# Window attention on one core: values multiplied over 128 rows of keys, and bands fetched at another place in the queue

## The chip, the core and the metric

The kernel runs on one core of a Trainium2 chip. Its time is the device time of one execution in microseconds (us); the time before is the median of three runs, 4207.44 us (4202.64 to 4210.01). A profile is one further execution with the hardware profiler on. Engines are named as in it: PE is TensorE's matmuls, PEld its weight loads, DVE is VectorE, ACT ScalarE, POOL GpSimd, and SP SyncE, which here only issues DMAs.

## What is computed

Two layers on `x` of 16 images, 56 x 56 pixels, 384 channels, all in float32. Cut to what matters:

```python
# layer 0: group norm, then shifted-window attention: windows of 7 x 7 pixels, 12 heads of 32 channels
qkv = roll(gn(x), (-3, -3)) @ w_qkv.T
score = einsum('bhwqd,bhwkd->bhwqk', q, k) / sqrt(32) + rel      # per window: 49 x 49
# the last row and the last column of windows: -inf between the shifted parts
out = einsum('bhwqk,bhwkd->bhwqd', softmax(score), v)
x = x + roll(out @ w_out.T + b_out, (3, 3))
# layer 1: group norm, then a 3 x 3 depthwise convolution with weights -1, 0 or 1
x = x + depthwise3x3(gn(x), sign(w))
```

## The kernel before, in words

**Strips and units.** An image is cut into 8 strips of 7 rows, which are 8 windows each (128 strips in all). A strip is two units of 4 windows, so there are 256 units. For each strip, TensorE multiplies the normalized input `xn` with the weights: queries and keys (`query_key`, L472), values (`value`, L485), and after attention the output projection (`project`, L656). Tokens lie along the free axis there, 392 at a time, and the shape is 128 x 128 weights. Results go to four PSUM banks (`bank`, L91) used in turn, and are copied out by ScalarE (L479, L492) or VectorE (L664).

**Attention of a unit.** The four windows are two pairs: `r` counts pairs, `w` the window in a pair. Window `w` of a pair has its keys in partitions 64 w to 64 w + 48. `scores` (L526) multiplies keys and queries, 48 matmuls of 32 rows; VectorE scales them and adds bias and mask into the tile `e` (`softmax`, L543); ScalarE makes the exponentials in place, with their sum along a row into `reach` for a later range check (`exponential`, L561). `add_up` (L597) sums over keys by a matmul with ones, `invert` makes the reciprocal on ScalarE and VectorE (L635 to L638), `attend` (L617) multiplies values and exponentials, one window and one head at a time, ScalarE copies the two banks `po` out (L627), and `divide` (L645) multiplies with the reciprocals. A float32 matmul is two passes in the records, each with its own weight load: the 48 matmuls of `attend` are 96 instructions.

```python
keys = slice(w * HT, w * HT + T)          # HT 64, T 49, D 32
nc.tensor.matmul(
    po[w][i * D : (i + 1) * D, (2 * j + r) * T : (2 * j + r + 1) * T],
    vs[s][keys, n * 2 + r, h * D : (h + 1) * D],
    by_head(u)[keys, i * NC + j, r] if fast else pts[u, j][keys, 2 * i + r, :],
```

The values get keys on partitions by 32 x 32 transposes on VectorE (`turn`, L496) and 16 DMAs a strip from SP (`by_key`, L508), which each carry a semaphore that the first matmuls of the strip wait for.

**The convolution** of image b - 1 runs beside the attention of image b. Its input goes to DRAM (`mid`, L680) and comes back in bands of 28 rows of one channel block, six to an image. For each band: `band` (L703) fetches it on SP into the one buffer `xb`; `pad` (L748) and `middle` (L778) on ScalarE normalize it into a padded tile and start the sum; eight `tap`s on VectorE (L784) add to it; `turn_sum` (L791) transposes, and eight `store`s (L798) send it from SP. The last image has no attention beside it: there a part of the channels is convolved on TensorE (`convolve`, L822, `carry`), the rest goes through `turn_late` (L855 to L863).

**The order.** Every engine takes its instructions in the order in which the program writes them. `all_units` writes, for each unit, six steps of large matmuls (`heavy`) with the attention's parts between them: `add_up`, `invert`, `attend` and `divide` after the first; `scores` and `softmax` of the next unit after the third or fourth (in the first or second unit of a strip), its `exponential` after the step that follows. All else has a due time in units (`at`), and is written when the unit comes to it. `plan_conv` gives the bands their due times: `step` is 2.6 units, `lead` is 3, and a band is due 0.75 steps before its first tap, its pad 0.35, its middle 0.25. One SP queue carries value loads, bands and stores in this order.

A second pass of the whole kernel, with `fast` false, runs only where the range check asks for it; it doesn't for these inputs.

Of the kernel before, what the change touches and what calls it, by code (L numbers as in the profile page):

```python
# [9 lines left out]
F32 = mybir.dt.float32  # L10
I32 = mybir.dt.int32
AF = mybir.ActivationFunctionType
# [22 lines left out]
def kernel(  # L35
# [55 lines left out]
    def bank(name):  # L91
        return ps.tile([P, 512], F32, tag="mm", name=name)
# [6 lines left out]
    ones = const.tile([P, P], F32, tag="ones", name="ones")  # L99

    least = const.tile([P, 1], F32, tag="least", name="least")
    reach = const.tile([P, 2, B * NU], F32, tag="reach", name="reach")
    seen = const.tile([P, B + NC], F32, tag="seen", name="seen")
    again = const.tile([P, 1], I32, tag="again", name="again")
    wq_t = const.tile([P, NC, 3 * C], F32, tag="wq", name="wq_t")
# [11 lines left out]

    xt = const.tile([P, NC, NR, D], F32, tag="xt", name="xt")

    es = const.tile([P, NH, 2, HT], F32, tag="e", name="e")  # L120

    hps = [const.tile([P, BR + 2, W + 2], F32, tag=f"hp{n}", name=f"hp{n}") for n in range(2)]

# [14 lines left out]
    def clear_more():  # L138
        nc.gpsimd.memset(power, -0.5)
        nc.gpsimd.memset(ones, 1.0)  # L140
        nc.gpsimd.memset(least, LEAST)
        nc.gpsimd.memset(seen, 0.0)
        for t in (qk[:, :, ST:], *hps, *accs):
            nc.gpsimd.memset(t, 0.0)
# [45 lines left out]
    def load_bias(queue, first_q, last_q, fast):  # L190


        if not loaded_bias:
            rel = ypool.tile([P, NC, WIN, R], F32, tag="y", name="rel").rearrange("q c h w -> q (c h w)")[:, : T * NH]
            nc.gpsimd.memset(rel, 0.0)
            loaded_bias.append(rel)
        rel = loaded_bias[0]
        flat = rel.rearrange("q (a n) -> q a n", a=WIN)
        for q in range(first_q, last_q):
            qr, qc = divmod(q, WIN)  # L200
            first = qr * REL + qc if fast else (WIN - 1 - qr) * REL + (WIN - 1 - qc)
            row = rel_table[first : first + 1, :]
            src = bass.AP(
                tensor=row.tensor,
                offset=row.offset,
                ap=[[NH, 1], [REL * NH, WIN], [1, WIN * NH]],
            )
            queue.dma_start(flat[q : q + 1], src)
        if last_q < T:
            return  # L210
        queue.dma_start(flat[HT : HT + T], flat[0:T])
        mask = ypool.tile([P, NC, WIN, R], F32, tag="y", name="mask").rearrange("q c h w -> q (c h w)")[:, : 2 * T]
        mask = mask.rearrange("q (v k) -> q v k", v=2)
        nc.gpsimd.memset(mask, 0.0)
        for w in range(2):
            queue.dma_start(mask[w * HT : w * HT + T], wmask[0:T, :, 0:T])
        loaded_bias.append(mask)
# [317 lines left out]
    def softmax(u, fast):  # L535

        s = u // UPS
        pp = raw[u]
        e = es.rearrange("k (i j) w q -> k i (j w) q", i=HPC)[:, :, :, :T]
        if fast:  # L540
            flat = es.rearrange("k h w q -> k (h w q)")[:, : NH * 2 * T]
            e = flat.rearrange("k (i n q) -> k i n q", i=HPC, q=T)
        nc.vector.scalar_tensor_tensor(  # L543
            e,
            pp[:, :, : NC * 2 * T].rearrange("q i (n k) -> q i n k", k=T),
            QSCALE,
            bias[:, int(s % NS == NS - 1)].rearrange("q (i j) w k -> q i (j w) k", i=HPC),
            ALU.mult,
            ALU.add,
        )  # L550
        if fast:
            return
        e = es.rearrange("q h w k -> q (h w) k")[:, :, :T]
        top = small.tile([P, 2 * NH], F32, tag="top", name=f"top_{u}")
        nc.vector.tensor_reduce(top, e, AX.X, ALU.max)
        nc.vector.tensor_tensor(e, e, top.unsqueeze(2).to_broadcast([P, 2 * NH, T]), ALU.subtract)

    def exponential(u, fast):
        if fast:
            flat = es.rearrange("k h w q -> k (h w q)")[:, : NH * 2 * T]  # L560
            nc.scalar.activation(flat, flat, AF.Exp, accum_out=reach[:, 0, u : u + 1])  # L561
            return
        e = es.rearrange("q h w k -> q (h w) k")[:, :, :T]
        nc.scalar.activation(e, e, AF.Exp)
        total = small.tile([P, 2 * NH], F32, tag="total", name=f"total_{u}")
        nc.vector.tensor_reduce(total, e, AX.X, ALU.add)
        inv = small.tile([P, 2 * NH], F32, tag="inv", name=f"inv_{u}")
        nc.vector.reciprocal(inv, total)
        nc.vector.tensor_tensor(e, e, inv.unsqueeze(2).to_broadcast([P, 2 * NH, T]), ALU.mult)
# [11 lines left out]
        nc.scalar.copy(pt, pp.rearrange("k (n q) -> k n q", q=HT)[:, :, :T])  # L581
        pts[u, j] = pt

    def by_head(u):

        flat = es.rearrange("k h w q -> k (h w q)")[:, : NH * 2 * T]
        return flat.rearrange("k (h r q) -> k h r q", h=NH, r=2)

    def add_up(u):

        e = by_head(u)
        su = raw[u][:, :, NC * 2 * T : NC * 3 * T]
        for r in range(2):
            for i in range(HPC):
                for w in range(2):
                    keys = slice(w * HT, w * HT + T)
                    nc.tensor.matmul(  # L597
                        su[i * D : (i + 1) * D, 2 * r + w].rearrange("p (j q) -> p j q", j=NC),
                        ones[keys, :D],
                        e[keys, i * NC : (i + 1) * NC, r],  # L600
                        start=True,
                        stop=True,
                    )
        sums[u] = su

    def attend(u, fast):
        s, n = divmod(u, UPS)
        if n == 0:
            ots[s] = two.tile([P, NC, ST], F32, tag="ot", name=f"ot_{s}")
        po = [bank(f"po_{u}_{w}") for w in range(2)]  # L610
        for j in range(NC):
            for r in range(2):
                for i in range(HPC):
                    for w in range(2):
                        h = HPC * j + i
                        keys = slice(w * HT, w * HT + T)
                        nc.tensor.matmul(  # L617
                            po[w][i * D : (i + 1) * D, (2 * j + r) * T : (2 * j + r + 1) * T],
                            vs[s][keys, n * 2 + r, h * D : (h + 1) * D],
                            by_head(u)[keys, i * NC + j, r] if fast else pts[u, j][keys, 2 * i + r, :],  # L620
                            start=True,
                            stop=True,
                        )
        ot = ots[s][:, :, n * UW * T : (n + 1) * UW * T]
        by_window = ot.rearrange("p j (r w q) -> p j r w q", r=2, w=2)
        for w in range(2):
            nc.scalar.copy(  # L627
                by_window[:, :, :, w, :], po[w][:, : NC * 2 * T].rearrange("p (j r q) -> p j r q", j=NC, r=2)
            )

    def invert(u):

# [169 lines left out]

    summed = {}

    def convolve(b, k, c):

        hp, _ = padded[b, k, c]
        pitch = W + 2
        both = pitch + W
        hp, acc = (a.rearrange("p h w -> p (h w)") for a in (hp, outs[b, k, c]))  # L810
        tiles = LR * W // OT
        summed[k] = []
        for first in range(0, tiles, 4):
            n = min(4, tiles - first)
            pc = bank(f"pc_{k}_{first}")
            summed[k].append((first, n, pc))
            for i in range(n):
                here = pc[:both, i * P : (i + 1) * P]
                row = 2 * (first + i)
                for t in (0, 1, 2, 3, 5, 6, 7, 8):  # L820
                    dy, dx = divmod(t, 3)
                    nc.tensor.matmul(  # L822
                        here,
                        hp[:, (row + dy) * pitch + dx : (row + dy) * pitch + dx + both],
                        late_tiles["dg"][:, t],
                        start=(t == 0),
                        stop=False,
                    )
                nc.tensor.matmul(here, acc[:, row * pitch : row * pitch + both], ident, start=False, stop=True)
# [35 lines left out]
    def plan_last(b, first):  # L865
# [8 lines left out]
        for n, (k, c) in enumerate(chunks):  # L874
# [11 lines left out]
                    at(when + 1.01 + 0.05 * part, store, b, k, c, part)  # L886
            else:
                for half in range(2):
                    at(when + 1.15 + 0.01 * half, turn_late, b, k, c, half, n == len(chunks) - 1)
            k, c = n, NC - 1  # L890
            at(when - 0.3 if n else when - 0.11, pad, b, k, c, True)
            at(when - 0.25 if n else when - 0.1, middle, b, k, c, True, n == 0)
            at(when + 0.1, convolve, b, k, c)
            at(when + 1.1, carry, b, k, c)


# [5 lines left out]
    def plan_conv(p, first, step, lead, late, queue):  # L902
# [5 lines left out]
        for n in range(NB * NC):  # L908
            k, c = divmod(n, NC)
            when = first + step * n  # L910
            at(when - 0.75 * step, band, p, k, c)
            at(when - 0.35 * step, pad, p, k, c)
            at(when - 0.25 * step, middle, p, k, c)
            for i, t in enumerate((0, 1, 2, 3, 5, 6, 7, 8)):
# [104 lines left out]
    with tc.manual_schedule():  # L1019
# [27 lines left out]


        worst = small.tile([P, 2], F32, tag="worst", name="worst")
        for n in range(2):  # L1050
            nc.vector.tensor_scalar(reach[:, n], reach[:, n], MOST[n], None, ALU.is_lt)
        nc.vector.tensor_reduce(worst[:, 0:1], reach.rearrange("p n u -> p (n u)"), AX.X, ALU.min)
        fine = small.tile([P, B + NC], F32, tag="fine", name="fine")
        nc.vector.tensor_scalar(fine, seen, 1.0e37, None, ALU.is_lt)
# [71 lines left out]
```

## Time and profile before

| | |
|---|---|
| median of 3 runs | 4207.44 us |
| the profiled execution: time, span | 4213.37 us, 4211.4 us |
| granted TensorE clock, mean | 0.988 |
| PE busy, in matmuls of L472, L485, L656 | 1587.0, 827.3, 816.2 us |
| PE busy, in matmuls of L526, L597 | 345.4, 188.8 us |
| DVE busy, in taps (L784) | 1378.5 us |
| DMA traffic | 439.45 MB, 104 GB/s |

A row of a group gives line, engine, operation, tiles written and read, shapes, the number of instructions, then busy time, mean duration of one in ns, and the engine's idle time just before them with what ended it. Passes of TensorE overlap, so busy time is less than number by duration. A row of waits gives who waited for whom, us in total, times, and the longest. A row of a timeline gives start, length, engine, line and what it does.

### The profile page before, as it was taken

To read this page: it belongs to the slowest core of one execution; us is meant where nothing else is said; L and a number is where in the kernel's file an instruction comes from. 1 tells how busy PE (TensorE), PEld (TensorE's weight loads), DVE (VectorE), ACT (ScalarE), POOL (GpSimd) and SP (SyncE) were. 2 spreads that over 40 slices of the span, in tenths; PEclk is the share of its full clock that TensorE was granted. 3 is DMA by queue.
4 is the path that set the end of the run, shared out by engine and by line. 5 is a ranking of instruction groups with operands and counts; after the bars stand their busy time and mean duration, and the time that the engine had idled before them with its cause. 6 is when DMAs were issued, how large, how long until landed. Compare 5 with 4: busy or idle time off the path is not lost.

```text
span 4211.4 us, 153120 instructions
## 1 busy us (share of the span) xinstructions
PE 4068.7 (97%) x67257; PEld 2565.1 (61%) x67257; DVE 3495.2 (83%) x3711; ACT 2232.3 (53%) x4654; POOL 1863.9 (44%) x3165
## 2 busy tenths in 40 slices
PE   5999999999999999999999999999999999999997
PEld 3666566565666666666566666666566566666656
DVE  3556889888898888889888888988989888888897
ACT  2545555555555555555555555655556555554552
POOL 5444435445453554445445453554445445451100
PEclk8999999999999999999999999999999999999998
DMA  4434555654565655556654565655555565554454
GB/s 92 79 63 85 97 107 116 112 111 92 111 122 93 124 109 101 99 106 117 112 115 97 103 121 93 124 112 99 98 112 112 109 121 96 102 119 83 96 109 107
DMA packets 1524021, 439.45 MB, mean 104 GB/s; under 512 B 1458970, under 2 KB 1473979, under 8 KB 1523346
## 3 DMA queue, kind: packets, MB, share of 16 engines
q1 hardware_dynamic: 1432680, 267.66, 37.3%
q0 software_dynamic: 87648, 159.12, 16.2%
q8 instruction: 532, 8.72, 0.9%
q10 hardware_dynamic: 3018, 2.78, 0.3%
q14 instruction: 143, 1.17, 0.1%
HBM read 169.63 MB, written 158.46 MB: 78 GB/s over the span
## 4 chain that ended last, share of the span: by engine, by line
PE 40%; issue 16%; DVE 14%; POOL 12%; DMA 10%; SPq 4%; ACT 3%; DVEq 0%; ACTq 0%; POOLq 0%
PE pq L472 16%; POOL xl L419 9%; PE pv L485 8%; PE py L656 8%; DVE o L784 6%; PE ps L526 3%; SPq L508 3%; PE po L617 3%; DMA xl<-in_x_dram 3%; DMA mid<-y 2%; PE ps L597 2%; DMA xb<-mid 2%; DVE e L543 1%; SPq L798 1%; DVE xt L436 1%
## 5 line engine op out<-in xcount | busy, mean ns | idle before, releaser
L472 PE MATMUL pq<-xn,wq_t 128*128 128x392 f32 x4608 | 1587.0, 497 | 0.3
L419 POOL DMA_DIRECT2D xl<-in_x_dram x1980 | 1332.8, 720 | 172.2 <-DMA mid<-y 59.6
L784 DVE SCALAR_TENSOR_TENSOR o<-hp,dw_t,o 128x1568 f32<-128x1568 f32 x752 | 1378.5, 1833 | 5.4
L472 PEld LDWEIGHTS pq<-xn,wq_t 128*128 128x128 f32 x4608 | 846.3, 188 | 596.6 <-issue 1.6
L485 PE MATMUL pv<-xn,wq_t 128*128 128x392 f32 x2304 | 827.3, 502 | 35.5 <-ACT vt L492 30.6
L656 PE MATMUL py<-ot,wo_t 128*128 128x392 f32 x2304 | 816.2, 499 | 15.1 <-DVE ot L645 15.1
L479 ACT COPY qk<-pq 128x392 f32<-128x392 f32 x768 | 369.2, 483 | 622.4 <-PE pq L472 621.2
L485 PEld LDWEIGHTS pv<-xn,wq_t 128*128 128x128 f32 x2304 | 425.9, 190 | 343.0 <-ACT vt L492 39.4
L676 POOL COPY y<-y 128x63 f32<-128x63 f32 x128 | 46.3, 362 | 1299.0 <-DVE y L664 1299.0
L656 PEld LDWEIGHTS py<-ot,wo_t 128*128 128x128 f32 x2304 | 426.3, 190 | 313.2 <-DVE ot L645 25.6
L637 DVE SCALAR_TENSOR_TENSOR ln<-ps,inv 128x588 f32<-128x588 f32 x256 | 195.3, 763 | 467.7 <-ACT inv L636 467.6
L561 ACT ACTIVATE e<-e 128x1176 f32<-128x1176 f32 x256 | 303.4, 1185 | 456.1 <-DVE e L543 454.2
L492 ACT COPY vt<-pv 128x392 f32<-128x392 f32 x384 | 188.9, 492 | 416.0 <-PE pv L485 415.4
L526 PEld LDWEIGHTS ps<-qk 32*64 32x64 f32 x24576 | 311.3, 132 | 156.5 <-issue 125.2
L617 PE MATMUL po<-e,v 49*32 49x49 f32 x24576 | 374.1, 212 | 12.3 <-DMA v<-vq 10.7
L617 PEld LDWEIGHTS po<-e,v 49*32 49x32 f32 x24576 | 362.6, 105 | 20.5 <-issue 10.2
L543 DVE SCALAR_TENSOR_TENSOR e<-ps,bias 128x1176 f32<-128x1176 f32 x256 | 347.7, 1358 | 17.2 <-PE ps L526 17.0
L526 PE MATMUL ps<-qk 32*64 32x49 f32 x24576 | 345.4, 226 | 9.0 <-issue 6.8
L448 ACT COPY x<-xt 128x196 f32<-128x196 f32 x720 | 225.8, 368 | 175.9 <-DVE xt L436 175.7
L496 DVE STREAM_TRANSPOSE vq<-vt 128x512 f32<-128x512 f32 x384 | 265.9, 694 | 9.6 <-ACT vt L492 6.5
L461 ACT ACTIVATE xn<-x,coef 128x392 f32<-128x392 f32 x384 | 247.1, 712 | 14.4 <-DMA coef<-cod 14.4
L664 DVE TENSOR_TENSOR y<-py,x 128x392 f32<-128x392 f32 x384 | 213.4, 556 | 44.7 <-PE py L656 44.1
(173 smaller groups left out, 3351.4 us busy)
## 6 DMA issues: line engine op xcount, KB each, us to landing
v<-vq SPq DMA_DIRECT2D x2048, 48.0 KB
xb<-mid SPq DMA_DIRECT2D x90, 855.5 KB
out_dram<-o SPq DMA_DIRECT2D x736, 98.0 KB
mid<-y POOLq DMA_DIRECT2D x112, 619.5 KB
xl<-in_x_dram POOLq DMA_DIRECT2D x1260, 52.5 KB
mid<-y POOLq DMA_DIRECT2D x15, 354.0 KB
xl<-in_x_dram POOLq DMA_DIRECT2D x180, 28.0 KB
mid<-y POOLq DMA_DIRECT2D x15, 265.5 KB
```

What stands on the lines that cost most here:

```text
L419: nc.gpsimd.dma_start(xz[i * D + lo : i * D + hi, c, k : k + n, :], flat[token : token + n * (hi - lo)].rearrange("(k t) c -> t k c", k=n) ...
L461: nc.scalar.activation(xn[:, c, :, :T], xs[s][:, c, :].rearrange("p (w t) -> p w t", t=T), AF.Identity, bias=coef[:, c, 1:2], scale=coef[: ...
L472: nc.tensor.matmul(pq[:, :ST].rearrange("p (w t) -> p w t", t=T), wq_t[:, c, m * P : (m + 1) * P], xn[:, c, :, :T], start=(c == 0), stop=( ...
L479: nc.scalar.copy(qk[:, m, :ST], pq[:, :ST])
L485: nc.tensor.matmul(pv[:, :ST].rearrange("p (w t) -> p w t", t=T), wq_t[:, c, 2 * C + m * P : 2 * C + (m + 1) * P], xn[:, c, :, :T], start= ...
L496: nc.vector.transpose(vq[:, :, :, m].rearrange("p h n d -> p n h d"), vt[:, m].rearrange("p (n w) (j b) -> p n (w j) b", w=2, b=D),)
L526: nc.tensor.matmul(pp[row * HT : (row + 1) * HT, i, k0 : k0 + T], qk[part, NC * fast + j, q0 : q0 + HT], qk[part, NC * (not fast) + j, q0 ...
L543: nc.vector.scalar_tensor_tensor(e, pp[:, :, : NC * 2 * T].rearrange("q i (n k) -> q i n k", k=T), QSCALE, bias[:, int(s % NS == NS - 1)]. ...
L561: nc.scalar.activation(flat, flat, AF.Exp, accum_out=reach[:, 0, u : u + 1])
L617: nc.tensor.matmul(po[w][i * D : (i + 1) * D, (2 * j + r) * T : (2 * j + r + 1) * T], vs[s][keys, n * 2 + r, h * D : (h + 1) * D], by_head ...
L656: nc.tensor.matmul(py[:, :ST], wo_t[:, c, m * P : (m + 1) * P], ots[s][:, c, :], start=(c == 0), stop=(c == NC - 1),)
L784: nc.vector.scalar_tensor_tensor(acc, by_half(hp[:, dy : dy + BR, dx : dx + W]), dw_t[:, c, t : t + 1], acc, ALU.mult, ALU.add)
```

## The change

Four things are changed; none touches the large matmuls.

1. The tile `e` grows from 12 x 2 x 64 to 12 x 2 x 2 x 49 numbers a partition. For each head and pair it has two halves, one for each window of the pair. `softmax` writes the scores into half 0. `exponential` makes two activations out of that, first into half 1, then in place into half 0, each with a bias `own` that is 0 in the partitions of the half's own window and -1e30 in the others, so that these become zero. The mask's rows that hold no key are -1e30 instead of 0, so their exponentials are zero too. `reach` gets a third column for the second accumulator.
2. `attend` multiplies all 128 rows of a pair's keys at once: 32 columns of values by 98 columns of exponentials, 24 matmuls instead of 48. A bank `po` then holds a pair, not a window. `add_up` still sums 49 rows at a time, from the half concerned.
3. `band` is due 1.22 steps before the first tap instead of 0.75, and not before `first - lead + 0.5`.
4. In the last image, `convolve` is written in two parts, at 0.1 and 0.4 of a chunk instead of both at 0.1, and `turn_late` at 1.3 instead of 1.15.

```diff
@@ exponential
-            flat = es.rearrange("k h w q -> k (h w q)")[:, : NH * 2 * T]
-            nc.scalar.activation(flat, flat, AF.Exp, accum_out=reach[:, 0, u : u + 1])
+            e = eb.rearrange("k (n w q) -> k n w q", w=2, q=T)
+            for w in (1, 0):
+                nc.scalar.activation(
+                    e[:, :, w],
+                    e[:, :, 0],
+                    AF.Exp,
+                    bias=own[:, w : w + 1],
+                    accum_out=reach[:, 2 * w, u : u + 1],
+                )
@@ attend
-        po = [bank(f"po_{u}_{w}") for w in range(2)]
+        po = [bank(f"po_{u}_{r}") for r in range(2)]
         for j in range(NC):
             for r in range(2):
                 for i in range(HPC):
...
+                    here = po[r][i * D : (i + 1) * D, 2 * j * T : 2 * (j + 1) * T]
+                    if fast:
                         nc.tensor.matmul(
+                            here,
+                            vs[s][:, n * 2 + r, value],
+                            by_head()[:, i * NC + j, r].rearrange("k w q -> k (w q)"),
                             start=True,
                             stop=True,
                         )
...
-        for w in range(2):
-            nc.scalar.copy(
-                by_window[:, :, :, w, :], po[w][:, : NC * 2 * T].rearrange("p (j r q) -> p j r q", j=NC, r=2)
-            )
+        for r in range(2):
+            nc.scalar.copy(ot[:, :, r], po[r][:, : NC * 2 * T].rearrange("p (j q) -> p j q", j=NC))
@@ add_up
-                        e[keys, i * NC : (i + 1) * NC, r],
+                        e[keys, i * NC : (i + 1) * NC, r, w],
@@ plan_conv
-            at(when - 0.75 * step, band, p, k, c)
+            at(max(when - 1.22 * step, first - lead + 0.5), band, p, k, c)
@@ plan_last
-                    at(when + 1.15 + 0.01 * half, turn_late, b, k, c, half, n == len(chunks) - 1)
+                    at(when + 1.3 + 0.01 * half, turn_late, b, k, c, half, n == len(chunks) - 1)
...
-            at(when + 0.1, convolve, b, k, c)
+            at(when + 0.1, convolve, b, k, c, 0)
+            at(when + 0.4, convolve, b, k, c, 1)
```

## The prediction

> **What bounds the kernel now.** I read the page's busy shares first, then its groups, the waits, and then the timelines of TensorE, ScalarE and SyncE around the longest waits.
>
> ```profile
> PE 4068.7 (97%) x67257; PEld 2565.1 (61%) x67257; DVE 3495.2 (83%) x3711; ACT 2232.3 (53%) x4654; POOL 1863.9 (44%) x3165
> ...
> L617 PE MATMUL po<-e,v 49*32 49x49 f32 x24576 | 374.1, 212 | 12.3 <-DMA v<-vq 10.7
> L561 ACT ACTIVATE e<-e 128x1176 f32<-128x1176 f32 x256 | 303.4, 1185 | 456.1 <-DVE e L543 454.2
> ```
>
> TensorE is the bound; a third engine at 83% has room. `attend` (L617) is 9% of its time, so halving its instructions can't move much more than that. The second place to look is where TensorE idles. The waits of all engines:
>
> ```profile
> ACT hp L748 <- DMA xb<-mid: 104.0, 16, 8.6
> ...
> PE pv L485 <- ACT vt L492: 30.6, 14, 2.7
> ...
> PE py L656 <- DVE ot L645: 15.1, 12, 3.0
> ```
>
> Sixteen times ScalarE waits for a band, some 7 us each, and 14 times a few us later TensorE waits for ScalarE's copy. Four consecutive strips (columns: length, then busy time of PE, PEld, DVE, ACT, POOL, TensorE's granted clock, DMA):
>
> ```profile
> 437.32:468.35 31.03, 30.99 (x537) 19.38 (x522) 29.18 (x31) 20.39 (x47) 15.33 (x23) 1.00 0.58 119
> 468.35:499.29 30.94, 30.94 (x536) 19.36 (x521) 29.61 (x33) 14.68 (x35) 29.60 (x51) 1.00 0.52 90
> 499.29:535.86 36.57, 33.00 (x537) 19.90 (x522) 28.23 (x32) 18.20 (x38) 8.68 (x20) 0.95 0.39 81
> 535.86:566.64 30.78, 30.78 (x536) 19.29 (x521) 24.93 (x25) 16.09 (x29) 13.62 (x22) 1.00 0.91 153
> ```
>
> The third strip is 5.6 us longer, and idles and runs at a lower clock. Measured between the starts of L617, the sixth strip of each of images 1 to 14 takes 34.5 to 36.6 us, the median strip 30.92. The excess of the 14 adds up to **62 us**. Its cause, ScalarE's timeline and then SyncE's:
>
> ```profile
> 496.29 0.19 ACT L561 ACTIVATION_READ_ACCUMULATOR e<-e 128x1 f32 x1
> 505.12 1.75 ACT L748 ACTIVATE hp<-xb,coef 128x1624 f32<-128x1624 f32 x1 [8.65 <-DMA xb<-mid]
> 506.78 0.47 ACT L492 COPY vt<-pv 128x392 f32<-128x392 f32 x1
> ```
> ```profile
> 482.70 6.47 SPq L508 DMA_DIRECT2D v<-vq  x8
> 489.21 2.69 SPq L798 DMA_DIRECT2D out_dram<-o  x4
> 491.95 5.76 SPq L508 DMA_DIRECT2D v<-vq  x8
> 498.20 0.36 SPq L703 DMA_DIRECT2D xb<-mid  x1
> ```
>
> The band stands behind 16 loads of values and 4 stores, is issued at 498.2 and lands 7 us later; the copy of `pv` stands behind the pad that waits for it.
>
> **What the skill says.** "TensorEngine Tiling (Array Packing)", Key Properties: a change of tiling mode drains TensorE; tiles work independently. The trace agrees: from the last start of L472 to the next line's first start is 329 ns where the shape stays 128\*128 and 420 where it changes, so 91 ns a change. "TensorE: Matmul & The Clock Gate", Part 3: three 32-column tiles side by side measured 2.38 times one; no matmul here is of full height and 32 columns. The same page, Part 1: idle TensorE falls to a lower clock; here 0.95 in the stalled strip against 1.00. "ScalarE: Activation LUTs", What ACT_TABLE_LOAD costs: a bias read by pointer adds some 93 ns; here L635 with one takes 753, L636 without 694, on the same shape: 59 ns, which I use.
>
> **The bands.** The fourth band of an image (n = 3) moves 0.47 steps = 1.22 units, some 19 us, earlier. In the built order of SP's queue it now stands ahead of those stores and loads. Before, 7 us were short; so ScalarE's wait goes, and with it nearly all of the 62 us. New: the band's DMA now waits on SP for ScalarE's `middle` of the band before (one buffer), which is emitted only 0.08 units earlier; stores and loads of values queue behind that. Values are issued 2.5 us or more before their use in most strips (median 5.6), 0.4 to 1.6 us in the sixth strip, whose loads stay behind stores as they were. I take **-56**; 62 is the most, 40 if half of the cover is used up by values arriving late.
>
> **The second exponential.** One costs 1.28 us (the accumulator is read 1.09 us after the start, for 0.19). The second adds 1.28, and two biases 0.12: 1.40 us a unit, 256 x 1.40 = 358 us of ScalarE, to 61%. What is on the path: I took, for every unit, the time from the end of L561 to the start of L597, which needs it. In units at the start of a strip the median is 2.4 us, 45 of 128 are under 1.4, and what they lack adds up to 13.1 us; in the other units 12 lack 12.8 us, but 10.4 of it follows band waits and goes with them. That leaves 15.5. Copies behind it on ScalarE: carrying 1.4 us through ScalarE's idle gaps, PSUM banks are late in 18 places, all just after band waits, so nothing. **+15**; between 5 and 45 if VectorE gets late too.
>
> **The product.** TensorE's timeline of one strip:
>
> ```profile
> 251.87 0.74 PE L597 MATMUL ps<-e,ones 49*32 49x147 f32 x32
> 252.40 1.66 PE L617 MATMUL po<-e,v 49*32 49x49 f32 x96
> ...
> 267.48 0.73 PE L597 MATMUL ps<-e,ones 49*32 49x147 f32 x32
> 268.01 1.19 PE L617 MATMUL po<-e,v 49*32 49x49 f32 x96
> ```
>
> Start to next start, L617 takes 1577 ns (median) in a strip's first unit and 1200 in its second, 48 matmuls of two passes each. Single records: eight tiles at once; in the second unit two passes start every 16.7 ns, 8 in 66.7, though a pass of 49 columns streams in about 41 (392 columns take 329), and where instructions had piled up behind a wait eight start in 48. So issue, not the array, holds this burst. In the first unit the first eight matmuls wait for the values' DMA semaphores, up to 125 ns apiece: the 377 ns.
> After: 24 matmuls, 48 passes of 98 columns, four tiles side by side. L597 shows a wave of 147 columns every 126 ns; 98 columns make 84. Twelve waves: 1.01 us, and 0.09 to the next shape: 1.10. The shape now also changes between L597 and L617: L597 grows from 531 to 452 + 126 + 91 = 669 ns. Four waits for eight: 190 of 377 ns. First unit: 669 + 1100 + 190 = 1.96 us against 2.11; second 1.77 against 1.73. A strip gains 0.11 us, 128 make 14; as waits overlap with waves, **-10**. Lower end, no drain between L597 and L617: 138 ns x 256 = 35 us more, -45. Upper end, weights not loaded behind a running pass: the first passes of L597 last 311 ns instead of 284, so 27 a wave, 12 x 27 x 256 = 83 us: +73. With no tiles side by side: 36 more waves, 36 x 84 x 256 = +774.
>
> **The rest at once.** VectorE writes runs of 49 in place of 1176 in a row, ScalarE's copies of `po` keep 294 elements, the sums L597 keep their 32 passes; nothing, hidden or equal. In the tail, the third chunk's transposes go ahead of half of the last convolution: its 8 stores (L863, 6.2 us of SP issue from 4193.1) come some 6 us earlier, ahead of the last ones: **-4**, from 0 to -5.
>
> **Sum** against the profiled execution (4213.37 us; span 4211.4): -56 + 15 - 10 - 4 = -55. The median of the three runs is 4207.44, 6 us lower: **4152**.
>
> **Rivals.**
> 1. The halved count pays in full (no drain): 4152 - 35 = 4117. For it: the burst is held by issue; against: 91 ns at every change of shape in this trace.
> 2. The gap fills: SP blocks on `middle`, or values come late in the strip freed. 45 of the 56 us are lost: 4197. For it: values there have 0.4 to 1.6 us; against: they keep their place and the band's transfer no longer sits beside them.
> 3. Slower: full-height weights can't be loaded behind a running pass of the same column tile: 4152 + 83 = 4235. It decides from 0.21 us a unit (55 / 256). For it: nothing here shows this shape; against: L597 and L472 load behind running passes.
> 4. The tiles don't run side by side: 4152 + 784 = 4936.
>
> **Chances.** Forecast 0.53 (its own range 4125 to 4190), rival 1 0.17, rival 2 0.12, rival 3 0.15, rival 4 0.03. About 0.2% (8.4 us) is what a measurement of this kernel can tell from no change. Faster: 0.53 + 0.17 and 0.08 of rival 2; the rest of rival 2 is even; rivals 3 and 4 are slower. The range runs from 4106, somewhat below rival 1 (-62 + 5 - 45 - 5 gives 4100, all at once), to 4222, which takes in +45 for the exponentials with -40 for the bands, and leaves out rivals 3 and 4.
>
> **What would show it.** Right: no wait of L748 for `xb`, sixth strips near 31 us; L617's line in about 1.1 to 1.3 us, 48 passes, starts 84 ns apart by tile; L597 waiting for the exponential some 60 times. Wrong: passes of `po` 111 or 336 ns apart by tile; or `xb` on time and the sixth strip still long.

## The result and the profile after

The changed kernel takes **4192.69 us** (median of 10 runs, 4189.18 to 4196.76) against 4207.03 us of 10 runs of the kernel before: a ratio of 0.9968, with a 95% interval of 0.9958 to 0.9977. That is 14 us faster. The forecast was 55 us faster. The profiled execution took 4196.76 us, with a span of 4195.0 us.

Lines of the page of the kernel after: the engines' busy times, the product, and the exponential. In the kernel after, `attend` is L630 (it was L617), the exponential L568 (L561), the sums over keys L609 (L597), the division L665 (L645) and the projection L676 (L656).

```profile
PE 4048.8 (97%) x54969; PEld 2467.9 (59%) x54969; DVE 3498.5 (83%) x3712; ACT 2591.4 (62%) x5166; POOL 1864.9 (44%) x3169
...
L568 ACT ACTIVATE e<-e,own 128x1176 f32<-128x1176 f32 x512 | 664.8, 1298 | 515.0 <-DVE e L549 505.7
...
L630 PE MATMUL po<-e,v 128*32 128x98 f32 x12288 | 325.1, 250 | 11.3 <-DMA v<-vq 11.2
```

The product has half the instructions (12288 for 24576) and 49 us less busy time (374.1 to 325.1). ScalarE has 359 us more (2232 to 2591), where the prediction had 358. Neither number is the answer: TensorE is busy 20 us less, and the time fell by 14.

The waits of all engines, the kernel after:

```profile
ACT ln L655 <- PE ps L609: 36.7, 126, 1.4
PE py L676 <- DVE ot L665: 36.4, 31, 2.1
PE ps L609 <- ACT e L568: 35.9, 58, 8.1
```

The wait of ScalarE for bands (104 us in 16 waits before) and the wait of TensorE behind it (30.6 us at L485) are gone. Two others have grown. The sums wait 58 times for the exponential, which was foreseen in its number ("some 60 times"). The projection waits 31 times for the division, 36.4 us against 15.1, and that was not foreseen. They are not the old waits grown longer: in images 1 to 14, 9 of the 12 stood in sixth strips before, behind the late bands; after, 14 of the 31 stand in third strips and 13 in second.

Windows of the strips two to four and of the sixth strip of image 4, the kernel after (columns as in the prediction: window, length, busy time of PE, PEld, DVE, ACT, POOL, clock, DMA share, GB/s):

```profile
1130.26:1162.55 32.29, 31.15 (x433) 18.59 (x425) 28.13 (x30) 21.44 (x45) 18.34 (x28) 1.00 0.69 129
1162.55:1195.51 32.96, 31.16 (x432) 18.57 (x425) 29.55 (x33) 23.23 (x51) 12.47 (x19) 1.00 0.62 122
1195.51:1226.90 31.39, 30.75 (x433) 18.57 (x425) 29.10 (x30) 22.13 (x47) 15.29 (x23) 1.00 0.55 119
...
1257.59:1289.30 31.71, 31.26 (x432) 18.76 (x424) 29.57 (x33) 20.43 (x42) 9.68 (x22) 1.00 0.55 108
```

The sixth strip is short now, and the second and third are long. Measured as in the prediction between starts of the product, over images 1 to 14, the mean lengths of the eight strips of an image are (us):

| strip | 1 | 2 | 3 | 4 | 5 | 6 | 7 | 8 |
|---|---|---|---|---|---|---|---|---|
| before | 30.97 | 31.18 | 30.80 | 31.17 | 30.81 | 35.35 | 31.09 | 30.91 |
| after | 31.01 | 32.10 | 33.32 | 31.22 | 30.72 | 31.77 | 30.64 | 30.64 |

Over the 14 images the sixth strips give back 50 us, the seventh and eighth 10, and the second and third take 48.

**Where the third strip stops.** The question is which chain of steps, through which engines, makes TensorE stop there, and how late that chain could be before it cost anything (its slack). ScalarE in the second unit of a third strip, first in the kernel before, then in the kernel after (a row is start, length, engine, line, tiles; in brackets the idle time before it):

```profile
1176.48 1.18 ACT L561 ACTIVATE e<-e 128x1176 f32<-128x1176 f32 x1 [1.21 <-DVE e L543]
...
1178.03 1.75 ACT L748 ACTIVATE hp<-xb,coef 128x1624 f32<-128x1624 f32 x1
...
1180.05 1.72 ACT L778 ACTIVATE o<-xb,cen 128x1568 f32<-128x1568 f32 x1
...
1182.03 0.77 ACT L635 ACTIVATE ln<-ps,least 128x588 f32<-128x588 f32 x1
```
```profile
1173.80 1.30 ACT L568 ACTIVATE e<-e,own 128x1176 f32<-128x1176 f32 x1 [1.85 <-DVE e L549]
1175.01 0.19 ACT L568 ACTIVATION_READ_ACCUMULATOR e<-e,own 128x1 f32 x1
1175.23 1.30 ACT L568 ACTIVATE e<-e,own 128x1176 f32<-128x1176 f32 x1
...
1176.89 1.76 ACT L768 ACTIVATE hp<-xb,coef 128x1624 f32<-128x1624 f32 x1
...
1178.92 1.70 ACT L798 ACTIVATE o<-xb,cen 128x1568 f32<-128x1568 f32 x1
...
1180.89 0.76 ACT L655 ACTIVATE ln<-ps,least 128x588 f32<-128x588 f32 x1
```

In both, the pad and the middle of a band stand in ScalarE's queue between the exponential and the reciprocal (`ln`), with three copies of queries and keys. Between the first start of the exponential and the start of `ln` lie 5.55 us before (1182.03 - 1176.48) and 7.09 after: 1.54 us more. What depends on `ln` comes next, on TensorE in the same two places (the queries and keys, the sums, the product, and the projection):

```profile
1180.61 0.73 PE L597 MATMUL ps<-e,ones 49*32 49x147 f32 x32
1181.14 1.27 PE L617 MATMUL po<-e,v 49*32 49x49 f32 x96
1182.34 4.22 PE L472 MATMUL pq<-xn,wq_t 128*128 128x392 f32 x12
1186.39 2.14 PE L656 MATMUL py<-ot,wo_t 128*128 128x392 f32 x6
```
```profile
1177.29 0.73 PE L609 MATMUL ps<-e,ones 49*32 49x147 f32 x32
1177.95 1.22 PE L630 MATMUL po<-e,v 128*32 128x98 f32 x48
1179.10 4.22 PE L479 MATMUL pq<-xn,wq_t 128*128 128x392 f32 x12
1185.00 2.24 PE L676 MATMUL py<-ot,wo_t 128*128 128x392 f32 x6 [1.68 <-DVE ot L665]
```

From the first of the twelve matmuls of queries and keys to the start of the projection it is 4.05 us before (1186.39 - 1182.34), and 5.90 after: TensorE reaches the projection and has nothing to multiply. The last step ahead of it is VectorE's division, which writes `ot`, before and after:

```profile
1185.33 0.77 DVE L645 TENSOR_TENSOR ot<-ot,ln 128x588 f32<-128x588 f32 x1
```
```profile
1184.18 0.77 DVE L665 TENSOR_TENSOR ot<-ot,ln 128x588 f32<-128x588 f32 x1
```

Before, the division ended about 0.3 us ahead of the projection, so the path had next to **no slack**. Of the lateness after, 1.54 us are the second activation, and 0.64 us are VectorE: measured from the sums back, the first exponential starts 3.49 us ahead of them instead of 4.13, since VectorE, which is busy without a gap there, wrote the scores later. Together 2.18, less 0.3 of slack, is 1.9, and the stop is 1.85 (5.90 - 4.05).

This is not one strip's accident. Take for each strip of images 1 to 14 the time at which the projection could have started, 329 ns after the last matmul of queries and keys, less the end of the division. Before, the median is 0.26 us in third strips, and 0.6 to 0.9 in the others, but for the sixth, where the bands make it 1.0 late. After, it is 1.8 us late in third strips and 0.7 in second ones.

### The profile page after: what moved, and what is told of

Same layout as the page of the kernel before. It is cut to its first block, busy times and chain, and to the rows that moved or that the text cites. A ratio compares the mean times of both kernels' runs of the same rounds, so it can differ in the third digit from the quotient of the medians.

```text
span 4195.0 us, 128983 instructions
## 1 busy us (share of the span) xinstructions
PE 4048.8 (97%) x54969; PEld 2467.9 (59%) x54969; DVE 3498.5 (83%) x3712; ACT 2591.4 (62%) x5166; POOL 1864.9 (44%) x3169
## 3 DMA queue, kind: packets, MB, share of 16 engines
q0 software_dynamic: 87648, 159.12, 15.5%
## 4 chain that ended last, share of the span: by engine, by line
issue 28%; PE 20%; POOL 19%; DVE 17%; DMA 9%; ACT 5%; SPq 1%; DVEq 0%; ACTq 0%; POOLq 0%
POOL xl L426 12%; PE pq L479 8%; DVE o L804 7%; PE pv L492 4%; PE py L676 3%; DMA mvd<-mv 3%; DVE e L549 2%; ACT e L568 2%; POOL dev L275 2%; DMA xl<-in_x_dram 2%; PE ps L533 2%; PE po L630 1%; DVE xt L443 1%; DMA gt<-mvd 1%; POOL mid L700 1%
## 5 line engine op out<-in xcount | busy, mean ns | idle before, releaser
L568 ACT ACTIVATE e<-e,own 128x1176 f32<-128x1176 f32 x512 | 664.8, 1298 | 515.0 <-DVE e L549 505.7
L676 PE MATMUL py<-ot,wo_t 128*128 128x392 f32 x2304 | 819.9, 501 | 36.4 <-DVE ot L665 36.4
L492 PE MATMUL pv<-xn,wq_t 128*128 128x392 f32 x2304 | 813.9, 497 | 1.6 <-ACT xn L468 1.2
L696 POOL COPY y<-y 128x63 f32<-128x63 f32 x128 | 58.7, 459 | 1388.0 <-DVE y L684 1388.0
L676 PEld LDWEIGHTS py<-ot,wo_t 128*128 128x128 f32 x2304 | 424.0, 190 | 343.2 <-DVE ot L665 63.0
L657 DVE SCALAR_TENSOR_TENSOR ln<-ps,inv 128x588 f32<-128x588 f32 x256 | 195.3, 763 | 363.2 <-ACT inv L656 363.0
L549 DVE SCALAR_TENSOR_TENSOR e<-ps,bias 128x1176 f32<-128x1176 f32 x256 | 347.3, 1357 | 12.1 <-PE ps L533 11.8
L630 PE MATMUL po<-e,v 128*32 128x98 f32 x12288 | 325.1, 250 | 11.3 <-DMA v<-vq 11.2
L459 DVE BATCH_NORM_STATS2 st<-x 128x6 f32<-128x392 f32 x360 | 200.2, 559 | 143.4 <-ACT x L458 143.4
L630 PEld LDWEIGHTS po<-e,v 128*32 128x32 f32 x12288 | 264.6, 110 | 75.0 <-issue 70.9
L455 ACT COPY x<-xt 128x196 f32<-128x196 f32 x720 | 225.6, 368 | 128.5 <-DVE xt L443 128.5
L503 DVE STREAM_TRANSPOSE vq<-vt 128x512 f32<-128x512 f32 x384 | 265.6, 693 | 8.7 <-ACT vt L499 5.1
```

Of the source, the lines that this page charges most:

```text
L492: nc.tensor.matmul(pv[:, :ST].rearrange("p (w t) -> p w t", t=T), wq_t[:, c, 2 * C + m * P : 2 * C + (m + 1) * P], xn[:, c, :, :T], start= ...
L503: nc.vector.transpose(vq[:, :, :, m].rearrange("p h n d -> p n h d"), vt[:, m].rearrange("p (n w) (j b) -> p n (w j) b", w=2, b=D),)
L549: nc.vector.scalar_tensor_tensor(e, pp[:, :, : NC * 2 * T].rearrange("q i (n k) -> q i n k", k=T), QSCALE, bias[:, int(s % NS == NS - 1)]. ...
L568: nc.scalar.activation(e[:, :, w], e[:, :, 0], AF.Exp, bias=own[:, w : w + 1], accum_out=reach[:, 2 * w, u : u + 1],)
L630: nc.tensor.matmul(here, vs[s][:, n * 2 + r, value], by_head()[:, i * NC + j, r].rearrange("k w q -> k (w q)"), start=True, stop=True,)
L676: nc.tensor.matmul(py[:, :ST], wo_t[:, c, m * P : (m + 1) * P], ots[s][:, c, :], start=(c == 0), stop=(c == NC - 1),)
```

## The experiments

Each kernel was run several times beside runs of the kernel before on the same chip. Differences are given against those runs, whose median was 4207.95 us for the first four told here, 4204.43 for the two that move the input or the middle, and 4211.18 for the rest. The 95% interval of such a difference is 3 to 6 us either way, so two kernels that lie less than some 8 us apart are not told apart by it.

**The bands alone.** The kernel before, with one line changed:

```diff
-            at(when - 0.75 * step, band, p, k, c)
+            at(max(when - 1.22 * step, first - lead + 0.5), band, p, k, c)
```

> The kernel before with the band fetch at its new due time as its only edit. Theory A (the changed kernel's parts are worth: bands -58 us, second exponential about +60, product about -27, tail -3): 4149 us, no wait of the pad for its band, sixth strips of an image near 31 us. Rival B (the early fetch gives most of its gain back, because SP blocks on the middle step or values come late; the exponential costs only about +15): 4180 to 4195 us, with waits of the product for values or of SP for ScalarE in their place.

Measured 4134.92 us, 73 less; ratio 0.9827 (0.9813 to 0.984). The sixth strip of image 4, the same kernel:

```profile
1239.59:1270.66 31.07, 31.00 (x537) 19.41 (x522) 29.07 (x32) 16.81 (x37) 10.50 (x23) 1.00 0.57 109
```

It took 34.54 us before. No wait for a band is left, and none of TensorE's took its place. The new wait that was foreseen is there, the band's fetch on SP for ScalarE's `middle`, but TensorE doesn't feel it; and of the projection's 12 waits for the division one is left:

```profile
SPq L703 <- ACT o L778: 189.4, 18, 17.8
```
```profile
PE py L656 <- DVE ot L645: 3.0, 1, 3.0
```

Over images 1 to 14 the sixth strips give 61 us, and the fourth, seventh and eighth 14 more. So the bands are worth more than forecast, and the whole change is 59 us slower than this one part of it.

**The change with the bands left where they were.** The same line the other way round in the kernel after.

> The changed kernel with the band fetch put back to its old due time. Theory A: 4193 + 58 = about 4250 us, slower than the kernel before. If the exponential had cost only the 15 us of the prediction and the product gained 10 to 27: 4190 to 4215 us.

Measured 4258.86 us, 51 more than before; ratio 1.0119 (1.0104 to 1.0135), which is 65 more than the whole change. Its waits:

```profile
ACT hp L768 <- DMA xb<-mid: 64.1, 13, 6.7
...
PE ps L609 <- ACT e L568: 46.5, 67, 8.1
...
PE py L676 <- DVE ot L665: 42.5, 42, 2.1
...
PE pv L492 <- ACT vt L499: 29.7, 14, 4.0
```

The bands' wait is back beside the two new ones. The rest of the change, taken alone, is a loss of 51 us.

**The product alone undone.** The kernel after with 48 matmuls of 49 rows a unit as before, and both exponentials kept:

```diff
...
-                            here,
-                            vs[s][:, n * 2 + r, value],
-                            by_head()[:, i * NC + j, r].rearrange("k w q -> k (w q)"),
+                            po[w][i * D : (i + 1) * D, (2 * j + r) * T : (2 * j + r + 1) * T],
+                            vs[s][keys, n * 2 + r, h * D : (h + 1) * D],
+                            by_head()[keys, i * NC + j, r, w] if fast else pts[u, j][keys, 2 * i + r, :],
...
```

The copies of `po` go by window again too.

> The changed kernel with the product put back to 48 matmuls over 49 rows; both exponentials stay. Theory A (128 rows are worth 27 us: 1.82 us against 2.11 and 1.73 for sums and product in a strip's first and second unit): 4193 + 27 = 4220 us, though less where ScalarE and not TensorE sets the pace: 4205 to 4220. Rival C (the product gains nothing or costs): 4193 us or below.

Measured 4207.80 us, as before; ratio 0.9999 (0.9991 to 1.0007). The product is worth 14 us in the changed kernel. Its line is that of the kernel before again:

```profile
L630 PE MATMUL po<-e,v 49*32 49x49 f32 x24576 | 369.0, 212 | 13.5 <-DMA v<-vq 12.3
```

**One exponential.** The kernel after without its activation into half 1, which holds ones written once at the start, so that the second window's half of every exponential is left out:

```diff
+        nc.vector.memset(eb, 1.0)
+        nc.vector.memset(reach, 1.0)
...
-            for w in (1, 0):
+            for w in (0,):
```

> The changed kernel without the second activation of the exponentials: the half for the second window of each pair is left out of the computation and holds ones written once. Theory A (the second exponential costs about 60 us, through ScalarE's chain from exponential over reciprocal to the division that the projection waits for): 4193 - 60 = about 4133 us, and the projection's waits for the division nearly gone. Rival B (its path cost is about 15): 4178 us.

Measured 4116.74 us, 91 less than before; ratio 0.9783 (0.9769 to 0.9796). Against the whole change that is 77 us for the second exponential, not 15. Both waits of TensorE are all but gone (the lines of this kernel stand two further down):

```profile
PE ps L611 <- ACT e L570: 6.6, 2, 6.3
...
PE py L678 <- DVE ot L667: 2.1, 1, 2.1
```

Against these, the whole change has 29 us more at the sums and 34 more at the projection, some 64 of the 77 us; where the other 13 lie was not traced. Strip by strip over images 1 to 14, the second exponential costs 20 us in second strips, 36 in third, 8 in fourth, 11.5 in sixth, 5 in first strips, and 2 in the other three together. It is not spread over all units; it is paid in few places.

**Pad and middle at another place.** If the cost is in what stands between exponential and reciprocal, it goes when that is moved, though ScalarE has the same work. The kernel after, with pads and middles written before the exponential of their unit:

```diff
+    def clear_of(when):
+        u = int(when)
+        edge = 0.66 if u % UPS else 0.49
+        return min(when, u + edge)
...
-            at(when - 0.35 * step, pad, p, k, c)
-            at(when - 0.25 * step, middle, p, k, c)
+            at(clear_of(when - 0.35 * step), pad, p, k, c)
+            at(clear_of(when - 0.25 * step), middle, p, k, c)
```

> The changed kernel with the due times of pad and middle moved earlier out of the stretch between an exponential and the next unit's reciprocal (from beyond 0.49 of a strip's first unit or 0.66 of its second back to that point); the same work on ScalarE. Theory A (the second exponential costs where pad and middle stand between it and the reciprocal; the third strip of an image is 2.6 us longer for that): about 4193 - 36 = 4157 us, third strips near 31 us. Rival D (it is ScalarE's load as such, wherever the pads stand): 4188 to 4198 us, the waits elsewhere.

Measured 4155.38 us, 56 less than before; ratio 0.9868 (0.9853 to 0.9883). TensorE's waits in it, and its second and third strips of image 4:

```profile
PE ps L609 <- ACT e L568: 26.9, 46, 7.5
...
PE py L676 <- DVE ot L665: 12.4, 17, 2.1
```
```profile
1122.38:1154.58 32.20, 31.06 (x432) 18.47 (x425) 28.03 (x30) 21.45 (x45) 18.51 (x29) 1.00 0.71 130
1154.58:1185.30 30.72, 30.72 (x433) 18.61 (x425) 30.14 (x34) 23.49 (x51) 12.71 (x20) 1.00 0.58 119
```

The third strip fell from 32.96 to 30.72 us with the same work on ScalarE (23.2 and 23.5 us), and third strips account for 36 of the 38 us that the strips of the 14 images lost. The projection's slack, worked out as above, goes from 1.8 us late to 1.0 to spare in third strips. The second strip did not move, and its projection is still 0.7 late. ScalarE at that place of a second strip, the same kernel, image 2:

```profile
635.48 1.29 ACT L568 ACTIVATE e<-e,own 128x1176 f32<-128x1176 f32 x1
...
637.14 0.63 ACT L455 COPY x<-xt 128x196 f32<-128x196 f32 x2
637.80 0.21 ACT L458 COPY x<-xt 128x21 f32<-128x21 f32 x1
...
638.30 0.62 ACT L455 COPY x<-xt 128x196 f32<-128x196 f32 x2
638.95 0.21 ACT L458 COPY x<-xt 128x21 f32<-128x21 f32 x1
...
639.44 0.75 ACT L655 ACTIVATE ln<-ps,least 128x588 f32<-128x588 f32 x1
```

Here it is not a band but the input of the next image (`arrange`, L455 and L458) that stands ahead of the reciprocal.

**The input moved too, and, in its place, less work for ScalarE.** Two kernels on top of the one just shown. In the first, `arrange` is written after the next unit's reciprocal where it would stand ahead of it, and the group norm that uses its sums follows 0.15 units later:

```diff
+    def past(when):
+        u = int(when)
+        edge = 0.66 if u % UPS else 0.49
+        return when if when < u + edge else u + 1.0
...
-                at(when + 0.2 + 0.2 * c, arrange, s, c)
+                at(past(when + 0.2 + 0.2 * c), arrange, s, c)
...
-        at(when + 0.8, norm_gather, (0, b), nc.gpsimd)
-        at(when + 0.9, norm_scale, (0, b), nc.gpsimd)
+        at(when + 0.95, norm_gather, (0, b), nc.gpsimd)
+        at(when + 1.05, norm_scale, (0, b), nc.gpsimd)
```

> This is the kernel with pad and middle put at another place, and in it the input of the next image (its copies on ScalarE, L455 and L458) is also put behind the reciprocal instead of between exponential and reciprocal. Theory A (place: what costs is ScalarE work that stands between the two exponentials and the reciprocal): in the trace of the kernel with only the pads moved, the second strips of an image still take 32.2 us where the kernel with one exponential takes 30.7, and there two such copies stand ahead of the reciprocal; 15 of these strips at 1.5 us make 23, and two thirds of the 0.4 us in first and fourth strips 8 more, so 4155 - 31 = 4124 to 4132. Rival E (load: ScalarE has too much to do, wherever it stands): no change, 4150 to 4158. If the input now comes late for the next image: above 4160.

In the second, `arrange` stays, and `middle` runs on GpSimd for all images but the last:

```diff
-        if first:
-            pool = nc.gpsimd if late else nc.vector
+        if first or not late and b < B - 1:
+            pool = nc.vector if first and not late else nc.gpsimd
```

> This is the kernel with pad and middle put at another place, and in it GpSimd computes the middle tap instead of ScalarE, for all images but the last. It takes 90 times 1.72 us = 155 us off ScalarE. Rival E (load): a third of the second exponential's added ScalarE time goes, so a third or more of the 38 us that are left, 4130 to 4143. Theory A (place): the middle no longer stands ahead of a reciprocal anyway, and the input copies do as before, 4150 to 4158. If GpSimd's own DMAs come late behind it: above 4160.

The first took 4136.86 us, 68 less than before; ratio 0.984 (0.9827 to 0.9854). The second took 4178.75, 26 less than before and so 30 more than with the middle on ScalarE; ratio 0.9938 (0.9924 to 0.9951). Second and fourth strip of image 4, the kernel with the input moved:

```profile
1114.72:1145.34 30.62, 30.62 (x433) 18.50 (x425) 25.26 (x28) 22.33 (x47) 18.51 (x29) 1.00 0.64 132
...
1176.08:1208.04 31.96, 30.72 (x433) 18.54 (x425) 29.29 (x31) 21.91 (x44) 15.25 (x24) 1.00 0.62 129
```

The second strip falls from 32.20 to 30.62 us: the place again. The projection waits for the division once in the whole run (2.2 us). The time is 5 to 13 us above the expectation (some 12 to 20 if counted from the runs of the kernel before, which were 7 us lower here), and one reason is the fourth strip, which grows from 31.02 to 31.96. There the sums now wait 1.2 us for the exponential, behind a copy of the input, a middle and a normalization in a row on ScalarE. The same row stands there in the kernel with only the pads moved, but TensorE came to it later. That gives back 12 us over the 14 images. Fourth strips hold 19 of the 25 us by which the 14 images stay above those with one exponential.

With the middle on GpSimd, ScalarE is busy 145 us less (2602 to 2458). The time grows all the same, above what either theory gave. The second strips are the test of the load: each of them has a middle that ScalarE no longer computes, and hardly anything else changes there. Image 4:

```profile
1128.72:1160.96 32.24, 31.09 (x432) 18.53 (x425) 27.91 (x30) 19.85 (x44) 19.96 (x29) 1.00 0.71 122
```

ScalarE has 19.85 us to do here instead of 21.45, and the strip takes 32.24 us instead of 32.20; the mean of the 14 stays at 32.10. So here it is not the load of ScalarE that costs. What grew in other strips, from the page of that kernel, and then VectorE and GpSimd in the sixth strip:

```profile
L804 DVE SCALAR_TENSOR_TENSOR o<-hp,dw_t,o 128x1568 f32<-128x1568 f32 x752 | 1419.4, 1888 | 4.2
```
```profile
1256.52 0.77 DVE L658 SCALAR_TENSOR_TENSOR ln<-ln,inv 128x588 f32<-128x588 f32 x1
1257.39 2.04 DVE L665 TENSOR_TENSOR ot<-ot,ln 128x588 f32<-128x588 f32 x1
```
```profile
1256.76 2.05 POOL L796 TENSOR_SCALAR o<-xb,cen 128x1568 f32<-128x1568 f32 x1
```

The taps take 1419.4 us instead of 1378.5, and a division that meets a middle on GpSimd takes 2.04 us instead of 0.77. The Trainium skill, "SBUF — State Buffer", section "SBUF: two separate sides", has a VectorE instruction with two inputs in SBUF and a GpSimd instruction that reads SBUF exclude each other at a port that they share. The trace agrees. The 57 taps that run beside a middle take 2543 ns on the mean, the other 695 take 1834; for L658 it is 1131 (34 of them) against 771, and for the division 1917 (17) against 771. All three have two inputs in SBUF. Those with one input in PSUM, or one input in all, don't grow: 1345 against 1358 ns for L549, 764 against 762 for L657, 688 against 693 for L503. The strips that grew most are the fourth (0.83 us), where L658 meets the middle 13 times, and the sixth (0.40), where the division does. In second strips only one such step is stretched in all 15 images. So this kernel's total says nothing of the load: it has a new delay on VectorE, in the steps from reciprocal to division among others.

**Without one of the two sums.** The kernel after, its activation into half 1 without `accum_out`, so that this half's part of the range check is left out. (The text below calls it the second activation, the one in place; the edit takes the sum from the first of the two.)

```diff
-                    accum_out=reach[:, 2 * w, u : u + 1],
+                    **({} if w else dict(accum_out=reach[:, 0, u : u + 1])),
```

> The changed kernel without the row sum of the second activation (the one in place): its part of the range check is left out of the computation. ScalarE is shorter by about 0.2 us a unit. If the path cost of the second exponential (76 us for some 1.5 us a unit) is in proportion to its length: 4193 - 10 = 4183 us. If it depends on whether ScalarE is late at all: 4193 us.

Measured 4187.67 us, 24 less than before; ratio 0.9946 (0.9933 to 0.996). That is 9 us less than the whole change, and 5 if the two medians are compared as they stand. The pair of activations gets only 0.09 us shorter, not 0.2 (medians of start to end 2.81 and 2.72): without the read between them, the second starts 1.33 us after the first instead of 1.42. An estimate of a saving in proportion, from these figures, is 77 x 0.09 / 1.54, some 5 us; the run agrees with that, but is too near to no gain at all to decide more.

**Bands and tail with the old product,** and the same with pads and middles moved as above (the one exponential of the kernel before in both).

> The kernel before with the new due time of the bands and the new order of the last image; old product, one exponential. Theory A: 4135 - 3 = 4132 us. If the tail's new order gains nothing: 4135 us.

> The same as the bands and the last image's order alone, with the due times of pad and middle moved as well. Theory A (with one exponential ScalarE is hardly late anywhere, so the place of the pads is worth nothing): 4128 to 4135 us. Rival D gives no difference either; a gain of over 10 us would say that ScalarE's chain costs time even with one exponential.

Measured 4132.76 us, ratio 0.9814 (0.9801 to 0.9827), and 4131.26 us, ratio 0.9813 (0.98 to 0.9826). The tail is worth 2 to 5 us over the bands alone. The intervals of the two runs overlap; in the traces, the time from the last product to the end goes from 106.5 to 104.8 us. The place of pads and middles, worth 41 us with two exponentials, is worth nothing that could be measured with one: with the bands alone, the projection's slack is 0.28 us in third strips and 0.6 or more in all others, and no strip is late. These two are the fastest kernels here that leave nothing out: the wide product never earns its exponential back in the orders tried (68 us less than before at best, against 78 and 80).

## Why the prediction was right in sign and wrong in size

In steps from kernel to kernel, each against the runs of the kernel before beside it: bands -73, tail on top of them -5 (-78 together), the wide product with one exponential on top of those -13 (-91), the second exponential +77. As these are steps from the kernel before to the kernel after, they must come to -14. The product step has the first exponential's new bias and layout in it (1.30 us instead of 1.18). Undone one at a time from the whole, bands, exponential and product are worth 65, 77 and 14 us.

| step | predicted | measured |
|---|---|---|
| bands | -56 | -73 (65 less in the changed kernel) |
| second exponential | +15 (5 to 45) | +77 |
| product | -10 (-45 to +73) | -13 and -14 |
| tail | -4 | -2 to -5 |
| sum | -55 | -14 |

The sign was right by luck. Had the bands brought the 56 us forecast for them, and not 73, the steps would come to 3 us slower, which is no change. Rival 2's 4197 us lies nearest to the result, by luck too: its mechanism did not occur.

**The step that failed** is the second exponential, in the sentence "Copies behind it on ScalarE: carrying 1.4 us through ScalarE's idle gaps, PSUM banks are late in 18 places, all just after band waits, so nothing." It followed the delay into one thing behind the exponential, the copies that free PSUM banks. It didn't follow it into the other: `ln` and `inv` on ScalarE, then three VectorE instructions, the last of which is the division that the projection multiplies. That path had some 0.3 us to spare in a third strip, and under 1 us in every other. The prediction put it at nothing; it measured 34 us of waiting at the projection. The lines that the prediction quotes name the path, as the projection waited 12 times, up to 3.0 us, for the division; but 9 of these waits were in sixth strips and 11 went with the bands, so they don't show how little slack the third strip had. Only the timelines do. The upper end of 45 was for VectorE being late, but not worked out from a path. The waits of the sums were counted with a method that was right in kind, 58 waits for "some 60", yet they came to 36 us of which 6 were there before, and 15.5 were expected. Two things that the sum left out make for this; how much each of them made was not measured. One is the length: two activations with their reads take 2.81 us (1173.80 to 1176.62) and not 1.28 + 1.40 = 2.68. The Trainium skill, "ScalarE: Activation LUTs", What ACT_TABLE_LOAD costs, has consecutive activations overlap by some 93 ns. These two don't: the second starts 1.43 us after the first, which takes 1.30. The read between them makes 0.09 us of that, by the run without it, and no overlap comes back when it goes. The other is VectorE, which stands 0.64 us later in the third strip.

**Bands.** The cause and its cure were right: the wait of L748 is gone, sixth strips stand at 30.98 us with the bands alone. All of the excess came back (61 of 62 us), so the 6 us that were held back for late values, and the fall to 40, did not come. 14 us more came from other strips. In the eighth, the first unit's product takes 1.23 us instead of 1.57, 4.8 of 5.4 us over 14 images, and so as much as a second unit's (1.20 before), which has no values to wait for; what helps the fourth and seventh strips was not traced.

**Product.** Right in kind. Sums and product, start to next shape, take 662 + 1162 ns in a first unit and 661 + 1153 in a second (medians). Predicted were 669 + 1100 + 190 for waits, and 669 + 1100. The drain between sums and product is there: 213 ns from the last start of L609 to the first of L630, against 79 before. Four passes start some 7 ns apart, and the next four 84 ns after those, as forecast. The first unit costs hardly more than the second (but for sixth strips, where values come late and it takes 1.81 us on the mean), so the 190 ns for the values' semaphores are not seen; that the drain covers them is the reading, not shown. By these medians a strip takes 0.20 us less instead of 0.11, 26 us over 128 strips. With the waits in them, sums and product together take 13 us less than with 49 rows and both exponentials (507.3 to 494.4), and 13 to 14 reach the time.

**Rivals.** 1 (no drain, 4117) fails on those 213 ns. 2 (the gap fills) fails on the bands alone: TensorE waits no longer for values than before (8.2 us against 10.7), and 73 us are gained. 3 (weights not loaded behind a pass) and 4 (tiles one after another) fail on the 84 ns between waves, where 111 and 336 would have shown. Most of the gain of the bands was lost again all the same, but in other strips and through a mechanism that none of the rivals had. A slower kernel, which the forecast thought possible through the product alone, was near through the exponential: without the bands the change is 51 us slower than before.

## What to carry to other kernels

Before work is added to an engine's queue, follow everything that the engine does behind it to the bound engine, through the other engines too, and write down the slack at the end of each such path. Here 1.5 us a unit on an engine that was idle for nearly half of the time cost 77 us, at the few places where other work stood between it and a result that was needed. A line of waits (15 us here) can name such a path, but its slack has to be read from the timeline. What stands in the queue between two steps of the path could here be moved with the same work on the engine, and gave 41 us back. Undoing one part at a time shows when a change with several parts is worth less than one of them.

## What the runs showed of the hardware

- Four full-height tiles of 32 columns run side by side with 98 columns each: starts 7 ns apart within a wave, waves 84 ns apart. "TensorE: Matmul & The Clock Gate", Part 3, models such a pack as one matmul and some 4 ns for each further tile; in a wave here it is 7.
- From the last start of 49-row tiles (L609) to the first of full-height tiles 213 ns pass, where 79 pass before, between two kinds of 49-row tiles; from full-height tiles of 32 columns to 128 columns 175 ns pass.
- Of two exponentials in a row, the second reading what the first read, the second starts 1.42 us after the first where the first one's sum is read between them, and 1.33 where it isn't; each takes 1.30.
- A VectorE instruction with two inputs in SBUF takes longer beside a GpSimd instruction that reads SBUF (a tap 2543 ns on the mean instead of 1834, the division up to 2242 instead of 771). One with a single input in SBUF doesn't (L549 1345 and 1358 ns).
